# Group norm's factor by Ln and Exp on ScalarE instead of Sqrt and VectorE's reciprocal, in a layer of linear attention with a new table of turns

## The chip, the cores and the metric

The kernel runs on one core of one Trainium2 chip. A core has TensorE (PE in the rows; PEld is its loading of weights), VectorE (DVE), ScalarE (ACT), GpSimd (POOL) and SyncE (SP), which only issues transfers here. The time is the device time of one execution in microseconds; the figure for a kernel is the median of its runs.

## What is computed

Eight sequences of 256 tokens and 512 channels (32 heads of 16) pass through one layer of the RWKV kind. Everything is float32. Cut to what matters:

```python
xn = ln(x);  sx = shift(xn) - xn
x5 = xn + sx * (maa_stack + tanh((xn + sx * maa_x) @ maa_w1) @ maa_w2)      # five mixes
w  = exp(-exp(time_decay + tanh(x5[1] @ decay_w1) @ decay_w2))
r, k, v, g = x5[3] @ Wr.T, x5[0] @ Wk.T, x5[2] @ Wv.T, silu(x5[4] @ Wg.T)
for t in range(256):                                # state s: 16 x 16 for each head
    a = k_t v_t;  out_t = r_t (u * a + s);  s = a + w_t * s
m, var = mean and variance of out over the 16 channels of a head
att = (out - m) * rsqrt(var + 1e-5) * gn_w + gn_b   # the group norm: this factor is changed
x = x + att * g @ Wo.T
xn2 = ln(x);  x = x + sigmoid(xr @ ffn_Wr.T) * (square(relu(xk @ ffn_Wk.T)) @ ffn_Wv.T)
```

## The kernel before, in words

Each sequence b goes through three stages: `inputs_of_scan` (norm, mixes, the projections r, k, v, g and the decay w), `scan`, and `rest` (group norm, Wo, second norm and the feed-forward part). Channels lie on the 128 partitions, time along the free axis. The 512 channels are four blocks; each block is scanned in four pieces of 128 x 1024 (L1003, on VectorE). For a piece, v is written to DRAM (`vo`, L920 and L976), read back spread over partitions (`vs`), multiplied by k (L1001 on VectorE, six of them at L998 on GpSimd), scanned into `st8` (in the rows `st`), and multiplied by r on GpSimd (L1006). Four pieces are then summed over the channels of a head by 32 matmuls (`gather`, L1014).

All operations are first recorded as a list in `Plan`, each with an engine, an estimated duration and the buffers that it writes and reads. What decides the order on every engine is `TURNS`, a table written out by hand or by a search: one number for each operation, and among the operations that are ready the one with the lowest number is taken next (`sequence` and `order`). The transfers, issued by SP in one queue, stand in that order too. So do the activation tables: `tables` walks through ScalarE's operations and puts a load (L1170) ahead of one whose function is not in the table that is in place. PSUM holds six tiles `ps`, and one tile `wrep` of twice their bytes; SBUF tiles such as `vs` (six) and `st8` (six) rotate, and an operation that needs one waits for its last reader.

The stage `rest` begins with the group norm. The squares of `att` (`sq`, L1032) are averaged over each head by eight matmuls into `pv` (L1040). Line 1045 takes the root of `pv` plus eps on ScalarE, line 1051 the reciprocal on VectorE, in place in the tile `rs`, which is the first `sq` tile. For seven of the eight sequences sixteen copies of 32 partitions (L1073) spread the factor over the partitions, and GpSimd multiplies `att` by it (L1076). For the last sequence eight matmuls do the spreading (L1059) and VectorE multiplies (L1067). Scale and bias (L1080), the product with g (L1083, L1085) and the matmuls with Wo follow. A branch under `kept`, which is False, is never built.

At the start of the program the weights for v are centred: eight groups of matmuls multiply the raw v weights (`Wraw`, two loads of 512 KB) by a centring matrix `cen` of 64 KB. `xin` is the first mix, `ta` the tanh of its projection, `psm` the four mixes that come from it.

Of the kernel before, what the change touches and what calls it, by code (L numbers as in the profile page):

```python
# [68 lines left out]
class Plan:  # L69
# [10 lines left out]
              "sqrt": "sqrt_and_others"}  # L80
# [40 lines left out]
    def stage(self):  # L121
# [160 lines left out]
    def order(self, phases):  # L282
# [8 lines left out]
        while queue:  # L291
# [21 lines left out]
            if op.engine == "ACT":  # L313
                if want == "tanh" and now in ("exp", "silu"):
                    want = now
                elif now == "tanh" and want in ("exp", "silu"):
                    mode["ACT"] = now = want
# [928 lines left out]
```

## Time and profile before

| what | value |
|---|---|
| median of 3 runs | 606.35 us (605.95 to 607.21) |
| span of the profiled execution | 607.4 us |
| PE busy | 596.5 us, 98% of the span |
| DVE busy | 539.7 us, 89% |
| ACT busy | 519.0 us, 85% |
| POOL busy | 511.6 us, 84% |
| table loads on ACT | 34 of 1283 ns |

The profiled execution's time is its span, 607.4 us; no other time of it is listed, and it lies 1.05 us above the median of the unprofiled runs. Busy time is the union of an engine's instructions. An engine that is busy all the time need not be at its best pace: PE also counts as busy when its clock is halved.

### The profile page before, as it was taken

Reading aid. Unit: us, or ns where it says so; the run is one execution under the profiler, and the core shown is the slowest. Engines: PE = TensorE matmul, PEld = TensorE weight load, DVE = VectorE, ACT = ScalarE, POOL = GpSimd, SP = SyncE. Lnnn points to the kernel's source line nnn. Section 1 sums busy time; section 2 is a strip of 40 time slices with the busy share of each in tenths; the row PEclk is TensorE's granted clock in tenths of the full one; section 3 lists DMA queues with packets and bytes.
Section 4 is the critical chain, followed back from the end, with each engine's and each line's share of the span. In section 5 each row is a group of like instructions: output and inputs, shape, how many; then the busy total and the mean of one; then the engine's idle time right before and its main releaser. Section 6 shows DMA issues by size and latency. Waiting matters only on the chain.

```text
span 607.4 us, 17029 instructions
## 1 busy us (share of the span) xinstructions
PE 596.5 (98%) x7022; PEld 346.3 (57%) x7022; DVE 539.7 (89%) x492; ACT 519.0 (85%) x1177; POOL 511.6 (84%) x405
## 2 busy tenths in 40 slices
PE   9999998899999999999999999999999999999997
PEld 7575655347634774446654584465744474546464
DVE  5789999799999999998899999999899999995342
ACT  5977879979999999989999999999998899968350
POOL 2989999989979999899989899988889798987020
PEclk9999999799999999999999999999999999999999
DMA  9887695649668789669767987788667878972352
GB/s 316 272 198 209 184 253 170 167 119 284 193 162 227 198 250 244 182 191 253 202 196 214 269 215 213 210 256 216 166 184 195 231 202 216 282 206 74 130 187 77
DMA packets 52638, 124.73 MB, mean 205 GB/s; under 512 B 5841, under 2 KB 11345, under 8 KB 52561
## 3 DMA queue, kind: packets, MB, share of 16 engines
q1 hardware_dynamic: 48048, 119.39, 70.3%
q10 hardware_dynamic: 4512, 4.26, 2.2%
q8 instruction: 55, 0.90, 0.7%
q14 instruction: 23, 0.18, 0.1%
HBM read 115.25 MB, written 8.39 MB: 204 GB/s over the span
## 4 chain that ended last, share of the span: by engine, by line
PE 68%; POOL 14%; ACT 7%; DVE 5%; DMA 3%; issue 2%; SPq 0%; ACTq 0%; DVEq 0%; POOLq 0%
PE ps L440 57%; POOL st L1006 7%; PE ps L1014 7%; POOL mix L822 3%; PE ps L658 2%; POOL vs L998 1%; DVE st L1003 1%; DMA vo<-v 1%; PE ps L862 1%; PE ps L564 1%; DMA x<-in_x 1%; DMA vs<-vo 1%; DVE vs L1001 1%; ACT xh L595 1%; POOL mix L850 1%
## 5 line engine op out<-in xcount | busy, mean ns | idle before, releaser
L1003 DVE TENSOR_TENSOR_SCAN st<-wrep,vs 128x1024 f32<-128x1024 f32 x128 | 287.9, 2273 | 7.1 <-PE ps L1014 3.5
L1006 POOL TENSOR_TENSOR st<-st,r 128x1024 f32<-128x1024 f32 x128 | 254.8, 2008 | 7.4 <-DVE st L1003 6.0
L1001 DVE TENSOR_TENSOR vs<-vs,ps 128x1020 f32<-128x1020 f32 x122 | 142.6, 1199 | 2.0 <-ACT ps L980 1.0
L440 PE MATMUL ps<-Ws,mix 128*32 128x512 f32 (+3 forms) x872 | 115.1, 585 | 0.0
L440 PEld LDWEIGHTS ps<-Ws,mix 128*32 128x32 f32 (+1 forms) x872 | 37.5, 116 | 63.1 <-issue 58.5
L822 POOL TENSOR_TENSOR mix<-mix,xn 128x512 f32<-128x512 f32 x62 | 66.9, 1103 | 4.1 <-DVE mix L806 4.0
L1014 PE MATMUL ps<-st,con 128*32 128x256 f32 x1024 | 63.7, 388 | 2.4 <-POOL st L1006 1.6
L440 PE MATMUL ps<-mix,Wv 128*32 128x256 f32 (+1 forms) x832 | 59.5, 380 | 1.2 <-DVE mix L819 1.0
L440 PE MATMUL ps<-mix,Wk 128*32 128x256 f32 (+1 forms) x856 | 59.8, 380 | 0.0
L440 PE MATMUL ps<-mix,Wr 128*32 128x256 f32 (+1 forms) x712 | 59.2, 380 | 0.0
L440 PE MATMUL ps<-mix,Wg 128*32 128x256 f32 (+1 forms) x544 | 58.1, 380 | 0.1
L440 PE MATMUL ps<-Ws,g 128*32 128x512 f32 (+1 forms) x416 | 58.1, 606 | 0.0
L440 PE MATMUL ps<-mix,Ws 128*32 128x256 f32 (+1 forms) x688 | 57.8, 380 | 0.0
L1014 PEld LDWEIGHTS ps<-st,con 128*32 128x32 f32 x1024 | 33.1, 111 | 30.0 <-issue 9.0
L440 PEld LDWEIGHTS ps<-mix,Wg 128*32 128x32 f32 (+1 forms) x544 | 42.2, 133 | 12.8 <-issue 0.7
L440 PEld LDWEIGHTS ps<-mix,Wv 128*32 128x32 f32 (+1 forms) x832 | 36.6, 116 | 22.4 <-issue 3.0
L440 PEld LDWEIGHTS ps<-mix,Ws 128*32 128x32 f32 (+1 forms) x688 | 39.6, 123 | 16.7 <-issue 1.4
L440 PEld LDWEIGHTS ps<-mix,Wr 128*32 128x32 f32 (+1 forms) x712 | 38.8, 122 | 16.9 <-issue 1.3
L440 PEld LDWEIGHTS ps<-mix,Wk 128*32 128x32 f32 (+1 forms) x856 | 37.0, 115 | 19.8 <-issue 2.2
L804 ACT ACTIVATE ps<-ps,vec 128x256 f32<-128x256 f32 x112 | 45.5, 448 | 2.9 <-PE ps L440 2.0
L1170 ACT ACT_TABLE_LOAD x33 | 42.3, 1283 | 0.6
L736 POOL TENSOR_TENSOR mix<-mix,sx 128x512 f32<-128x512 f32 x28 | 35.5, 1279 | 6.6 <-ACT mix L729 3.7
(143 smaller groups left out, 1000.4 us busy)
## 6 DMA issues: line engine op xcount, KB each, us to landing
vs<-vo SPq DMA_DIRECT2D x128, 512.0 KB, 5.2
Ws<-in_wo SPq DMA_DIRECT2D x16, 512.0 KB, 5.4
Ws<-in_fk SPq DMA_DIRECT2D x16, 512.0 KB, 5.5
Ws<-in_fr SPq DMA_DIRECT2D x16, 512.0 KB, 5.7
Ws<-in_fv SPq DMA_DIRECT2D x16, 512.0 KB, 5.3
x<-in_x SPq DMA_DIRECT2D x9, 512.0 KB, 6.0
vo<-v ACTq DMA_DIRECT2D x15, 256.0 KB, 5.4
out<-o SPq DMA_DIRECT2D x15, 256.0 KB, 3.8
```

The costliest lines, as they stand in the source:

```text
L440: nc.tensor.matmul(out[i : i + n], lhsT=w[:, i : i + n], rhs=x, start=first, stop=final)
L564: nc.tensor.matmul(ps()[:, 0, :], lhsT=warm[:, 0, 0:P], rhs=warm[:, 0, 0:T], start=True, stop=True)
L595: summed(junk[n], mv, [src[n]], lambda n=n: nc.scalar.activation(junk[n](), src[n](), AF.Copy, accum_out=mv()[:, n, 0:1]), 0)
L658: nc.tensor.transpose(to[:, m, n * P : (n + 1) * P], xh[n]()[:, k * P : (k + 1) * P], idt())
L736: gp(512, t, [t, u], lambda t=t, u=u: nc.gpsimd.tensor_tensor(t(), t(), u(), ALU.add))
L804: act(256, p_, [p_, vec], lambda g=g, q=q, m=m, p_=p_: nc.scalar.activation(p_()[:, m, :], p_()[:, m, :], AF.Identity, bias=col(f"maa_{g}" ...
L822: gp(512, t, [t, xn[q]], lambda q=q, t=t: nc.gpsimd.tensor_tensor(t(), t(), xn[q]()[:, :, 1 : T + 1], ALU.add))
L1001: dve(4 * T, [vs], [vs, kp], lambda m=m, vs=vs, kp=kp: nc.vector.tensor_tensor(vs()[:, :, 1:T], vs()[:, :, 1:T], kp()[:, m : m + 1, 1:T].t ...
L1003: dve(4 * T, [st], [w, vs, first], lambda w=w, vs=vs, st=st: nc.vector.tensor_tensor_scan(st().rearrange("p n t -> p (n t)"), w().rearrang ...
L1006: gp(4 * T, st, [st, r], lambda m=m, st=st, r=r: nc.gpsimd.tensor_tensor(st(), st(), r()[:, m : m + 1, :].to_broadcast([P, 4, T]), ALU.mul ...
L1014: nc.tensor.matmul(pat()[32 * i : 32 * i + 32, 0, :], lhsT=con()[:, s : s + 32], rhs=done[i]()[:, j, :], start=(j == 0), stop=(j == 3),)
L1170: nc.scalar.preload_act_table_set(op.table)
```

## The change

Lines 1045 to 1051 become two activations on ScalarE. The first is the logarithm of the variance plus eps, the second the exponential of -0.5 times it, in place. Both are marked "ln", whose table `natural_log_exp_and_others` also serves a later `exp`, and two lines in `order` and `tables` let an `exp` keep that table when it is in place. VectorE's reciprocal of 128 x 256 goes, eight of them. The dead branch `kept` goes. All of `TURNS` is replaced, so the order of work changes on every engine and in SP's queue. ScalarE's program holds 34 table loads before and after.

```diff
     TABLES = {"exp": "exp_and_others", "tanh": "exp_and_others", "silu": "silu_and_others", "sig": "sigmoid_and_others",
-              "sqrt": "sqrt_and_others"}
+              "sqrt": "sqrt_and_others", "ln": "natural_log_exp_and_others"}
...
     TURNS = """
-        8 72 12 20 41 124 40 135 48 116 79 78 141 119 3 32 84 31 128 181 183 185 11 10 19 39 62 68 36 65 69 37
...
@@ in order
                 elif now == "tanh" and want in ("exp", "silu"):
                     mode["ACT"] = now = want
+                elif want == "exp" and now == "ln":
+                    want = now
@@ in tables
                 want = "silu" if want == "silu" else "exp"
+            elif want == "exp" and mode == "ln":
+                want = mode
@@ in rest
         act(256, rs, [pv, eh], lambda: nc.scalar.activation(
-            rs()[:, 0:T], pv()[:, 0, :], AF.Sqrt, bias=eh()[:, 0:1]), "sqrt", 1)
-        kept = False
-        if kept:
-            dve(256, [pv], [rs], lambda: nc.vector.reciprocal(pv()[:, 0, :], rs()[:, 0:T]), 6.25)
-        else:
-            dve(256, [rs], [rs], lambda: nc.vector.reciprocal(rs()[:, 0:T], rs()[:, 0:T]), 6.25)
+            rs()[:, 0:T], pv()[:, 0, :], AF.Ln, bias=eh()[:, 0:1]), "ln", 1)
+        act(256, rs, [rs], lambda: nc.scalar.activation(rs()[:, 0:T], rs()[:, 0:T], AF.Exp, scale=-0.5), "ln")
```

Three places show what the new turns move. The first is PE's order near the start, some 9 to 14 us into the run. `Ws_168` is the centring matrix, `Ws_169` the second half of the raw v weights; `mix_109` and `mix_110` are the two halves of `xin`, and the rows that read `ta_123` are the four mixes. Before:

```order
L440 MATMUL ps_177<-Ws_168,Ws_169 128x128 x2
L440 MATMUL ps_176<-Ws_168,Ws_169 128x128 x2
L440 MATMUL ps_173<-mix_109,mw_66 128x256 x2
L440 MATMUL ps_173<-mix_110,mw_66 128x256 x2
L440 MATMUL ps_174<-Ws_168,Ws_169 128x128 x2
L440 MATMUL ps_173<-ta_123,mw2a 128x256
```

And now, in the changed kernel, at the same place:

```order
L444 MATMUL ps_176<-Ws_168,Ws_169 128x128 x2
L444 MATMUL ps_177<-Ws_168,Ws_169 128x128 x2
L444 MATMUL ps_175<-Ws_168,Ws_169 128x128 x2
L444 MATMUL ps_173<-mix_109,mw_66 128x256 x2
L444 MATMUL ps_173<-mix_110,mw_66 128x256 x2
L444 MATMUL ps_173<-ta_123,mw2a 128x256
```

The last centring group moved from behind the projection of `xin` to ahead of it. In SP's queue, the load of the centring matrix moved too: it stood right behind the first half of the raw v weights, and it now stands behind the vectors `vec` and the initial state `s` of the second sequence.

The second place is GpSimd's order where the first scans arrive, 33 to 47 us into the run. `sx` are the differences of neighbouring tokens for the third sequence, `st` the scanned pieces of the first, `vs` the one piece that GpSimd multiplies by k. Before:

```order
L935 TENSOR_TENSOR rk_153<-r_128,k_125 128x512
L1006 TENSOR_TENSOR st_155<-st_155,r_128 128x1024
L690 TENSOR_TENSOR sx_106<-xn_101 128x512
L998 TENSOR_TENSOR vs_150<-vs_150,k_125 128x4x255
L1006 TENSOR_TENSOR st_156<-st_156,r_128 128x1024
L690 TENSOR_TENSOR sx_105<-xn_102 128x512
L822 TENSOR_TENSOR mix_120<-mix_120,xn_104 128x512
```

And now:

```order
L939 TENSOR_TENSOR rk_153<-r_128,k_125 128x512
L1010 TENSOR_TENSOR st_155<-st_155,r_128 128x1024
L694 TENSOR_TENSOR sx_105<-xn_102 128x512
L694 TENSOR_TENSOR sx_106<-xn_101 128x512
L1010 TENSOR_TENSOR st_156<-st_156,r_128 128x1024
L1002 TENSOR_TENSOR vs_151<-vs_151,k_125 128x4x255
L1010 TENSOR_TENSOR st_157<-st_157,r_128 128x1024
```

The second `sx` and one `st` moved ahead of `vs`. In SP's queue the second load of the g weights moved behind seven of the first eight `vs` transfers.

The third place is PE's order at the last group norm, about 559 to 568 us. `L1040` and `L1044` are the averages into `pv`, `L1059` the spreading of the factor, the rows that read `Ws_168` with a `mix` are the feed-forward projection of the sequence before. Before:

```order
L1040 MATMUL ps_173<-sq_162,con 32x256 x2
L440 MATMUL ps_175<-Ws_168,mix_117 32x512 x8
L440 MATMUL ps_175<-Ws_169,mix_119 32x512 x8
L1059 MATMUL ps_173<-sq_161,con 128x256
L1059 MATMUL ps_172<-sq_161,con 128x256
```

And now:

```order
L1044 MATMUL ps_177<-sq_161,con 32x256 x2
L444 MATMUL ps_173<-Ws_168,mix_114 32x512 x8
L1059 MATMUL ps_177<-sq_162,con 128x256
L1059 MATMUL ps_172<-sq_162,con 128x256
L444 MATMUL ps_173<-Ws_170,mix_110 128x512 x2
```

One half of that projection moved from between the averages and the spreading to behind the spreading. A little later, the two halves of the last sequence's Wo product for its first 128 tokens now follow one another, where before they alternated with the second 128 tokens.

## Rows read from the trace of the kernel before

**Rows 1.** The page: busy time, share of the span and instructions of each engine.

```profile
PE 596.5 (98%) x7022; PEld 346.3 (57%) x7022; DVE 539.7 (89%) x492; ACT 519.0 (85%) x1177; POOL 511.6 (84%) x405
```

**Rows 2.** Stretches of 15 us: busy us by engine, granted clock, DMA share, GB/s.

```profile
0.00:15.00 15.00, 13.78 (x86) 11.76 (x90) 8.44 (x24) 8.19 (x19) 4.02 (x20) 1.00 0.92 315
...
90.00:105.00 15.00, 13.15 (x232) 7.90 (x228) 15.00 (x14) 13.90 (x30) 15.00 (x12) 1.00 0.70 197
105.00:120.00 15.00, 12.23 (x190) 6.51 (x184) 10.81 (x11) 14.21 (x33) 15.00 (x10) 0.85 0.58 147
...
255.00:270.00 15.00, 15.00 (x216) 6.89 (x212) 13.08 (x12) 13.32 (x32) 14.97 (x11) 1.00 0.65 186
```

**Rows 3.** PE's waits, whole run: for whom, us in total, times, longest.

```profile
PE ps L440 <- ACT k L901: 1.2, 1, 1.2
```

**Rows 4.** Groups by line: shapes, count, busy us, mean ns, idle before.

```profile
L1170 ACT ACT_TABLE_LOAD x33 | 42.3, 1283 | 0.6
...
L1051 DVE RECIPROCAL sq<-sq 128x256 f32<-128x256 f32 x8 | 13.9, 1736 | 2.5 <-ACT sq L1045 2.5
...
L1045 ACT ACTIVATE sq<-ps,eh 128x256 f32<-128x256 f32 x8 | 3.8, 474 | 0.3 <-PE ps L1040 0.3
L781 ACT ACTIVATE ta<-ps 128x256 f32<-128x256 f32 x8 | 3.0, 380 | 1.6 <-PE ps L440 1.6
```

**Rows 5.** PE's instructions in order of time, start: start, duration, idle before.

```profile
8.01 3.36 PE L440 MATMUL ps<-Ws,Ws 128*128 128x128 f32 x28
11.20 1.96 PE L440 MATMUL ps<-mix,mw 128*128 128x256 f32 x8
13.00 0.61 PE L440 MATMUL ps<-Ws,Ws 128*128 128x128 f32 x4
13.63 1.15 PE L440 MATMUL ps<-ta,mw2a 32*128 32x256 f32 x16
```

**Rows 6.** SP's transfers in order of time: start and duration of the issue.

```profile
2.10 0.47 SPq L429 DMA_DIRECT2D Ws<-in_consts  x1
2.61 0.43 SPq L429 DMA_DIRECT2D vec<-in_vecs  x1
...
4.07 1.05 SPq L429 DMA_DIRECT2D s<-in_state  x1
...
24.05 14.35 SPq L429 DMA_DIRECT2D vs<-vo  x8
```

**Rows 7.** Transfers, whole run: size, median us from issue to landing.

```profile
Ws<-in_consts SPq DMA_DIRECT2D x1, 64.0 KB, 5.2
```

**Rows 8.** POOL's instructions in order of time, 36 to 47 us.

```profile
38.70 2.37 POOL L998 TENSOR_TENSOR vs<-vs,k 128x1020 f32<-128x1020 f32 x1 [1.44 <-DMA vs<-vo]
41.02 2.00 POOL L1006 TENSOR_TENSOR st<-st,r 128x1024 f32<-128x1024 f32 x1
42.98 1.05 POOL L690 TENSOR_TENSOR sx<-xn 128x512 f32<-128x512 f32 x1
```

**Rows 9.** A stretch of 2 us around PE's wait for POOL, columns as above.

```profile
116.00:118.00 2.00, 1.74 (x20) 0.82 (x24) 0.81 (x3) 1.98 (x7) 2.00 (x3) 0.50 1.02 242
```

**Rows 10.** PE in order of time: first g projection, two summing groups, a Wo product.

```profile
47.90 5.39 PE L440 MATMUL ps<-mix,Wg 128*32 128x256 f32 x96
53.11 1.91 PE L1014 MATMUL ps<-st,con 128*32 128x256 f32 x32
...
116.26 3.64 PE L1014 MATMUL ps<-st,con 128*32 128x256 f32 x32 [1.59 <-POOL st L1006]
119.67 8.32 PE L440 MATMUL ps<-Ws,g 128*32 128x512 f32 x64
```

**Rows 11.** PE in order of time, at the last group norm and after.

```profile
559.62 3.62 PE L440 MATMUL ps<-Ws,mix 128*32 128x512 f32 x32
563.17 1.13 PE L1059 MATMUL ps<-sq,con 64*128 64x256 f32 x8
...
578.89 1.09 PE L658 MATMUL ps<-idt,xh 128*128 128x128 f32 x8 [0.40 <-DVE xh L628]
```

More of the change, by code (lines that the diff above doesn't have):

```diff
@@ L1072, in rest @@
                         rows = slice(32 * i, 32 * i + 32)
-                        act(335 if kept else 376, rsb, [pv if kept else rs], lambda blk=2 * q + n, n=n, rows=rows, rsb=rsb: nc.scalar.copy(
-                            by_block(rsb)[rows, n, :],
-                            (pv()[:, 0, :] if kept else rs()[:, 0:T])[32 * blk : 32 * blk + 32, :]))
+                        act(376, rsb, [rs], lambda blk=2 * q + n, n=n, rows=rows, rsb=rsb: nc.scalar.copy(
+                            by_block(rsb)[rows, n, :], rs()[32 * blk : 32 * blk + 32, 0:T]))
                 gp(512, att, [att, rsb], lambda att=att, rsb=rsb: nc.gpsimd.tensor_tensor(
```

269 rows, old and new, of the table TURNS are left out of this document.

## Prediction

> **What bounds the kernel now.** I read the page's busy times first. PE is busy for 596.5 us, DVE for 539.7, ACT for 519.0 and POOL for 511.6 [rows 1]. The span is 607.4 us, so PE is idle for 10.9 us in all, and work taken from another engine can give back at most what PE waits for it, or what PE loses to its clock. So the next question is where PE's idle time lies, and the stretches of 15 us answer it. In the long middle PE is busy for all 15.00 us of a stretch while DVE has 13.08 and ACT 13.32 [rows 2]: there PE is the bound. In the first stretch PE lacks 1.22 us, and from 90 to 120 us it lacks 1.85 and 2.77 us, while POOL is busy for all of 30 us [rows 2]: in the first fifth of the run POOL's queue paces PE. The list of waits names what is left: PE's wait at the summing group at 116.26 us is for POOL, 1.59 us long [rows 10], and one of 1.2 us is for an evacuation by ACT [rows 3]. Behind the wait at 116 us comes a second loss. The granted clock is 0.50 there, the lower level of 1.2 GHz [rows 9]; the 32 matmuls take 3.64 us where the same group took 1.91 us, and the 64 behind them 8.32 us [rows 10] where 32 of that shape take 3.62 us [rows 11], so 2 x 3.62 = 7.24. The lower clock costs 1.73 + 1.08 = 2.8 us.
>
> **What the change removes.** Eight reciprocals of 1.736 us, 13.9 us of DVE [rows 4]. On the path I count them at nothing: in the middle PE's own work covers them, and in the stretch from 90 to 120 us it is POOL that is full. If DVE were the engine waited for, they would give up to 13.9 us, but DVE is the releaser of no wait of PE of that size, and after 116 us PE has no idle time to give.
>
> **What it adds.** Eight exponentials of 128x256 on ACT. No row shows this one; the nearest are the tanh of the same shape at 0.380 us and the root at 0.474 us [rows 4], and I take 0.38, since the tanh too has no pointer for its bias: 3.0 us of ACT's 607. The step from variance to factor shrinks from 0.474 + 1.736 us on two engines to 0.474 + 0.38 on one. Queued behind the exponential on ACT stand a table load and then copies out of PSUM that PE waits for. I take nothing for it, because PE's work covers ACT's 13.32 of 15 us [rows 2]; without that cover seven exponentials in the middle would cost 7 x 0.38 = 2.7 us. That end is kept for the range.
>
> **Table loads.** A load takes 1.283 us [rows 4], and the built programs hold 34 before and after, since a tanh follows the new pair and wants the other table back. So the term is nothing. The Trainium skill (ScalarE: Activation LUTs, section "Table sets: the hidden batching unit") says that a logarithm followed by an exponential needs one load where an exponential and a root need two. By that rule ACT would lose eight loads, 10.3 us, and the third rival below would fall away; by the order of this kernel it loses none, and no run shows otherwise yet.
>
> **The new turns, start.** At 8.01 us PE begins the centring of the v weights; 28 of its matmuls stand before the projection of xin at 11.20 us, four behind it, and the tanh of that projection releases the four mixes at 13.63 us [rows 5]. Now all 32 stand before it. From 8.01 to 11.20 us is 3.19 us for 28, so 3.65 for 32: the projection, and all that follows from it, starts 0.46 us later. That is the lower end. The centring matrix is also issued later. Before, its issue was at 2.10 us [rows 6] and it landed 5.2 us later [rows 7], at 7.3, before PE asked for it. Now the issues of vec (0.43) and of the state (1.05) [rows 6] go first: about 3.65, landing at 8.85, so 0.84 us behind 8.01. Upper end 1.3 us. The state's 1.05 us may be less in a queue that is less full, so I take the middle, +0.9 us. Behind the delayed mixes stand the projections of v, its way through DRAM, and the first scans.
>
> **The new turns, POOL.** At 38.70 us POOL has waited 1.44 us for a transfer of vs [rows 8]. The row at 42.98, an sx of 1.05 us, and the st at 41.02, 2.0 us [rows 8], now go ahead of that vs, so the transfer may land some 3 us later before POOL waits. Gain 1.44 us, at least 1.05 if the st is late itself; I take 1.44, since the 3 us of work that go ahead of vs are twice the gap. POOL then stays full until 120 us [rows 2], the work ahead of the summing group at 116 us is the same set of instructions on POOL and on PE in both kernels, and so this group starts 1.44 - 0.9 = 0.54 us earlier, with PE's wait before it and the lower clock behind it unchanged. After it PE is the bound and carries the 0.54 us to the end.
>
> **Transfers that move.** The second half of the g weights goes behind seven vs transfers, issued by 24.05 + 14.35 = 38.4 us at the latest [rows 6]. Its first reader is at 47.90 us [rows 10], 9.5 us later, and the one landing shown here took 5.2 [rows 7]. Nothing, and at most a wait of PE at that place, which POOL's pace would swallow until 116 us.
>
> **The new turns, end.** Between the last averages and the spreading stood two halves of a projection, 3.62 us of PE [rows 11], enough to hide the root and the reciprocal (2.2 us). Now one half, 1.8 us, stands there and 0.85 us of ACT are to be hidden: no wait, no gain, since the other half only moves. At 578.89 us PE waits 0.40 us for the normed tokens [rows 11]. The first 128 tokens' Wo product is now finished before the second's begins, so one of the two statistics is out of the way early: I take the 0.40 us, between 0 and 0.4.
>
> **Sum.** +0.9 - 1.44 - 0.40 = -0.94 us: 606.5 in the profiled span. The span of before lies 1.05 us above the median of 606.35, and I move the median by the same sum: **605.4 us**. With the ends of the terms: 0.46 - 1.44 - 0.40 = -1.4 and 1.3 - 1.05 - 0 = +0.25, so 605.0 to 606.6.
>
> **Rivals.** First, the clock does not fall. PE's idle time around 114 us is made of waits for ACT and for POOL; if the new order splits it so that the granted clock stays at 2.4 GHz, the 2.8 us come back: 605.4 - 2.8 = 602.6. For it speaks that both waits lie in one short stretch and any shift of ACT's evacuations divides them anew; against it that their sum is set by POOL, which has the same work. The Trainium skill (TensorE: Matmul & The Clock Gate, Part 1) says that the moment at which the clock switches varies from run to run of the same kernel. By that rule a run could come out at this rival's 602.6 without any cause in the program; the one trace here shows one fall after a wait, which agrees, and cannot show the variation.
>
> Second, the start costs its upper end and POOL gains nothing, because the first scans come 1.3 us late and POOL, which now wants two of them before vs, waits for DVE instead of for the transfer: +1.3 - 0.4 = +0.9, 607.2. Against it: DVE loses work at the same time only later, but its first multiplication waits for a transfer that is no longer behind the g weights.
>
> Third, on the other side: the exponentials come to stand in front of PSUM copies that PE needs. PE already waited 1.2 us for ACT at one such copy [rows 3]. If seven exponentials each reach PE with their 0.38 us, 605.4 + 2.7 = 608.1. It decides from the point where PE waits for ACT at six of the seven places (6 x 0.38 = 2.3 us takes 605.4 past 607.6). Against it: DVE's results reach ACT 1.36 us sooner at the same places.
>
> **How the numbers follow.** I give the forecast 0.50, the clock 0.20, the lost POOL gain 0.13, the ACT waits 0.17. A change of 0.2%, 1.2 us, is about what a measurement of this kernel can tell from none; that is 605.1 and 607.6. Within 0.2%: the lost gain and two thirds of the forecast, 0.46. Faster: the clock and one third of the forecast, 0.37. Slower: the ACT waits, 0.17. The range reaches to the clock's 602.6 and the ACT waits' 608.1, which leaves out about one in ten on either side; the forecast's own is 605.0 to 606.6.
>
> **What the changed profile would show.** The mixes' first matmuls at about 14.5 us instead of 13.63; no wait of POOL for the transfer near 38 us; the summing group now at 116.26 at about 115.7 us, with a clock of 0.50 behind it; no RECIPROCAL of 128x256, and an exponential near 0.38 us; 34 table loads; no wait at the last transposes. The prediction is wrong if the clock column has no 0.50 near 116 us or has a second one, or if PE's waits for ACT after 130 us add up to more than 1 us.

## The result, and the profile after

The changed kernel takes 608.34 us in the median of 5 runs (608.07 to 609.51); the kernel before took 606.16 us in 5 runs of the same comparison (605.9 to 607.21). The ratio is 1.0037, with a 95% interval of 1.0021 to 1.0052: the change makes the kernel 2.2 us slower, where 1 us faster was forecast.

The two profiled spans hide this, 607.4 us before and 607.7 after. In every execution that lists both, the time is 1.8 us more than the span, so the profiled execution of before would have been listed at 609.2 us, 2.9 above the median that the prediction was made from. It was an unlucky one, and that matters below. One execution of the run e4 below was in a slower state (626.87 us at a granted clock of 0.949) and is left out of its figures.

The page's busy times of the changed kernel, against [rows 1]:

```profile
PE 594.6 (98%) x7250; PEld 347.1 (57%) x7250; DVE 530.8 (87%) x484; ACT 522.5 (86%) x1185; POOL 512.2 (84%) x405
```

DVE loses 8.9 us and ACT gains 3.5. The groups by line answer to [rows 4] (count, busy us, mean ns, idle before):

```profile
L1169 ACT ACT_TABLE_LOAD x33 | 42.3, 1283 | 0.6
L1049 ACT ACTIVATE sq<-ps,eh 128x256 f32<-128x256 f32 x8 | 3.8, 474 | 0.1
L1051 ACT ACTIVATE sq<-sq 128x256 f32<-128x256 f32 x8 | 3.3, 416 | 0.2
```

No load is added, the logarithm costs what the root cost, and the exponential 0.416 us where 0.38 was forecast. Of these, nothing explains a loss. The stretches of 15 us of the changed kernel, columns as in [rows 2], say where to look:

```profile
45.00:60.00 15.00, 13.34 (x244) 8.10 (x237) 13.60 (x14) 9.94 (x22) 15.00 (x12) 1.00 0.80 229
60.00:75.00 15.00, 15.00 (x278) 12.11 (x272) 13.96 (x10) 12.78 (x26) 12.67 (x9) 1.00 0.70 187
...
105.00:120.00 15.00, 12.36 (x206) 8.26 (x202) 12.56 (x12) 14.29 (x34) 15.00 (x11) 0.92 0.71 179
```

The same two stretches of the kernel before:

```profile
45.00:60.00 15.00, 14.87 (x272) 8.78 (x268) 15.00 (x14) 10.62 (x24) 15.00 (x13) 1.00 0.79 214
60.00:75.00 15.00, 15.00 (x276) 9.10 (x272) 15.00 (x11) 13.42 (x28) 15.00 (x10) 1.00 0.65 173
```

The prediction has POOL full up to 120 us. It is not: from 60 to 75 us POOL is busy for 12.67 of 15.00 us, and from 45 to 60 us PE for 13.34, where it had 14.87. POOL's instructions of the changed kernel in order of time (start, duration, idle before) show the wait of [rows 8] gone, and two new ones:

```profile
40.48 2.39 POOL L1002 TENSOR_TENSOR vs<-vs,k 128x1020 f32<-128x1020 f32 x1
...
60.08 2.02 POOL L1002 TENSOR_TENSOR vs<-vs,k 128x1020 f32<-128x1020 f32 x1
63.30 1.09 POOL L972 TENSOR_TENSOR att<-v,att 128x512 f32<-128x512 f32 x1 [1.20 <-ACT att L967]
...
71.54 3.96 POOL L1010 TENSOR_TENSOR st<-st,r 128x1024 f32<-128x1024 f32 x2 [1.12 <-DVE st L1007]
```

Each is followed back one step. ACT's instructions of the changed kernel:

```profile
53.99 0.30 ACT L998 ACTIVATE vs<-s,cm 128x4 f32<-128x4 f32 x1 [2.55 <-DMA vs<-vo]
54.19 0.58 ACT L984 COPY ps<-k 128x512 f32<-128x512 f32 x1
54.79 1.28 ACT L1169 ACT_TABLE_LOAD   x1
56.09 1.08 ACT L935 ACTIVATE g<-ps 128x512 f32<-128x512 f32 x2
```

ACT stands still for 2.55 us before an instruction of 0.30 us that writes four columns of a vs tile, because that tile's transfer has not landed. Behind it in ACT's queue stand a copy, a table load and both evacuations of g, and, later, the copies of att for which POOL waits at 63.30. In the kernel before, the write of this piece stood behind both evacuations. The wait at 71.54 comes by way of DVE, whose instructions of the changed kernel show two waits in a row, the second for a transfer:

```profile
59.16 4.47 DVE L1007 TENSOR_TENSOR_SCAN st<-wrep,vs 128x1024 f32<-128x1024 f32 x2 [1.40 <-ACT vs L998]
64.68 2.34 DVE L1005 TENSOR_TENSOR vs<-vs,ps 128x1020 f32<-128x1020 f32 x2 [1.04 <-DMA vs<-vo]
66.94 4.46 DVE L1007 TENSOR_TENSOR_SCAN st<-wrep,vs 128x1024 f32<-128x1024 f32 x2
```

The transfers that SP issues in the changed kernel at that time (start of the issue, duration):

```profile
49.40 1.80 SPq L433 DMA_DIRECT2D vs<-vo  x3
51.25 0.58 SPq L433 DMA_DIRECT2D x<-in_x  x1
51.92 0.42 SPq L433 DMA_DIRECT2D Ws<-in_wo  x1
55.60 6.41 SPq L433 DMA_DIRECT2D vs<-vo  x2
```

A load of x and one of half of Wo now stand ahead of the vs transfer that is issued at 55.60 us and for which DVE waits until 64.68. The kernel before issued an x load ahead of 39 us and its first Wo load behind 73 us.

PE's instructions of the changed kernel show what arrives there, against [rows 5] and [rows 10]:

```profile
13.97 1.15 PE L444 MATMUL ps<-ta,mw2a 32*128 32x256 f32 x16 [0.68 <-ACT ta L785]
...
56.78 1.93 PE L1018 MATMUL ps<-st,con 128*32 128x256 f32 x32 [1.66 <-POOL st L1010]
...
117.55 3.53 PE L1018 MATMUL ps<-st,con 128*32 128x256 f32 x32 [1.28 <-POOL st L1010]
```

The summing group that stood at 116.26 us stands at 117.55, where 115.7 was forecast. From the terms: 0.34 for the start, -1.44 for the wait of POOL that went, 1.20 + 1.12 for those that came, gives +1.22 us, and 1.29 are measured, with the same set of instructions on POOL up to the group's last piece in both programs. (The wait at 56.78 is put down to POOL, but its pieces were done at 47.8 us. The program gives this group the PSUM tile of the first g projection, and ACT empties that from 56.09 on: this is ACT's late evacuation again. By PE's wait ACT's copies of att come late, and so POOL's wait at 63.30.)

### The profile page after: what moved, and what is told of

It reads as the page before. It is cut to its first block, busy times and chain, and to the rows that moved or that the text cites. A ratio compares the mean times of both kernels' runs of the same rounds, so it can differ in the third digit from the quotient of the medians.

```text
span 607.7 us, 17471 instructions
## 1 busy us (share of the span) xinstructions
PE 594.6 (98%) x7250; PEld 347.1 (57%) x7250; DVE 530.8 (87%) x484; ACT 522.5 (86%) x1185; POOL 512.2 (84%) x405
## 4 chain that ended last, share of the span: by engine, by line
PE 71%; DVE 13%; POOL 7%; DMA 3%; ACT 2%; issue 2%; SPq 0%; DVEq 0%; ACTq 0%; POOLq 0%
PE ps L444 60%; PE ps L1018 7%; DVE st L1007 6%; DVE vs L1005 4%; POOL st L1010 4%; DMA vs<-vo 3%; PE ps L662 2%; DVE mix L810 2%; PE ps L866 1%; POOL mix L826 1%; POOL vs L1002 1%; DMA xt<-in_x 1%; DVE x L1090 0%; PE ps L1044 0%; ACT L1169 0%
## 5 line engine op out<-in xcount | busy, mean ns | idle before, releaser
L444 PEld LDWEIGHTS ps<-mix,Wv 128*32 128x32 f32 (+1 forms) x856 | 37.9, 115 | 20.0 <-DVE mix L823 1.6
L444 PEld LDWEIGHTS ps<-mix,Ws 128*32 128x32 f32 (+1 forms) x784 | 37.8, 118 | 19.2 <-issue 1.4
L810 DVE TENSOR_TENSOR mix<-ps,sx 128x512 f32<-128x512 f32 x56 | 36.3, 678 | 4.2 <-ACT ps L808 2.7
```

Of the source, the lines that this page charges most:

```text
L444: nc.tensor.matmul(out[i : i + n], lhsT=w[:, i : i + n], rhs=x, start=first, stop=final)
L810: dve(512, [t], [p_, sx[q]], lambda q=q, t=t, p_=p_: nc.vector.tensor_tensor(t(), p_(), sx[q](), ALU.mult))
```

## The experiments

`MOVED` in the diffs gives an operation, named by its number in `TURNS`, another number; a fraction puts it between two others.

| run | what it is | median, us (runs) | ratio to before, 95% interval | median of the runs at granted clock 1.00 (runs) |
|---|---|---|---|---|
| e1 | arithmetic alone, old turns | 613.76 (5) | 1.0110 (1.0094 to 1.0127) | 612.4 (2) |
| e2 | new turns alone, old arithmetic | 632.55 (4) | 1.0430 (1.0413 to 1.0447) | none |
| e3 | changed kernel, ACT's write later | 608.92 (9) | 1.0039 (1.0023 to 1.0056) | 608.0 (3) |
| e4 | e3, and the loads put back | 606.98 (11) | 1.0002 (0.9987 to 1.0016) | 605.8 (5) |
| e5 | the loads put back alone | 607.62 (12) | 1.0012 (1.0000 to 1.0025) | 607.1 (8) |
| e6 | kernel before again | 607.14 (12) | 1.0003 (0.9988 to 1.0018) | 605.0 (1) |
| e7 | kernel before with both faults | 607.33 (12) | 1.0006 (0.9989 to 1.0023) | 605.7 (2) |
| e8 | old turns, copies for reciprocals | 608.03 (12) | 1.0017 (1.0000 to 1.0033) | 605.9 (3) |
| e9 | changed kernel again | 609.05 (10) | 1.0047 (1.0030 to 1.0064) | 608.3 (3) |
| e10 | e4, and PE's start put back | 606.82 (12) | 0.9999 (0.9986 to 1.0013) | 606.0 (5) |
| e11 | e10, and three of POOL's later | 607.04 (12) | 1.0009 (1.0000 to 1.0018) | 606.9 (4) |
| e12 | kernel before, POOL's step alone | 607.15 (12) | 1.0015 (0.9999 to 1.0031) | 605.3 (1) |

The kernel before took 606.52 us in the comparison of e1 to e4 (20 runs), 606.83 in that of e5 to e8 (35), 606.39 in that of e9 to e11 (27) and 606.45 in that of e12 (17). Its runs at a granted clock of 1.00 had medians of 605.5 (7), 605.8 (9), 605.6 (7) and 604.9 us (6) in these four.

### Arithmetic and turns apart: e1 and e2

e1 is the change without its lines of `TURNS`:

```diff
-            rs()[:, 0:T], pv()[:, 0, :], AF.Sqrt, bias=eh()[:, 0:1]), "sqrt", 1)
-            dve(256, [rs], [rs], lambda: nc.vector.reciprocal(rs()[:, 0:T], rs()[:, 0:T]), 6.25)
+            rs()[:, 0:T], pv()[:, 0, :], AF.Ln, bias=eh()[:, 0:1]), "ln", 1)
+        act(256, rs, [rs], lambda: nc.scalar.activation(rs()[:, 0:T], rs()[:, 0:T], AF.Exp, scale=-0.5), "ln")
```

> The logarithm and the exponential in the order of the kernel before. In that order five more table loads fall on ACT (38 in place of 33, because the roots of the layer norms shared the root's table with the group norm): ACT gets 5 x 1.28 + 8 x 0.4 = 9.6 us more, DVE 13.9 us less. Theory (the loss comes from the new turns between 50 and 75 us): the arithmetic moves the time by less than 0.2%, 605.0 to 607.4, and POOL still waits about 1.4 us for a transfer near 38.7 us. Rival (the exponentials, or the loads, stand in front of PSUM copies that PE needs): 608 or more, with PE's waits for ACT adding up to more than 1 us behind 130 us.

613.76 us, 7.2 above the kernel before: the theory, that the arithmetic moves the time by less than 0.2%, falls, and the rival came (PE's waits for ACT behind 130 us add up to 4.2 us). The groups by line of this run count five loads more:

```profile
L1169 ACT ACT_TABLE_LOAD x38 | 48.8, 1283 | 0.6
```

and its stretch from 300 to 480 us, columns as in [rows 2], shows PE without work for 5.4 us of 180, where the second trace of the kernel before has 179.92 us of work:

```profile
300.00:480.00 180.00, 174.62 (x2166) 98.74 (x2161) 163.21 (x136) 168.87 (x380) 159.64 (x124) 1.00 0.75 208
```

The reason that the expectation gives for the five loads, a table shared with the layer norms' roots, is not the right one: in the kernel before each of the eight roots of the group norm has a load of its own. ACT's instructions of e1 show what happens (L1049 is the logarithm, L1051 the exponential, L1108 a tanh):

```profile
301.00 0.47 ACT L1049 ACTIVATE sq<-ps,eh 128x256 f32<-128x256 f32 x1
...
301.88 1.28 ACT L1169 ACT_TABLE_LOAD   x1
303.18 1.09 ACT L1108 ACTIVATE o<-ps 128x512 f32<-128x512 f32 x2
304.28 1.28 ACT L1169 ACT_TABLE_LOAD   x1
305.57 0.42 ACT L1051 ACTIVATE sq<-sq 128x256 f32<-128x256 f32 x1
```

In the old order a tanh stands between the two steps at three of the eight places (the others at 380 and 444 us), so the table is changed there and back, which makes five loads more in all. At 309.09 us PE then waits 1.40 us for the next tanh on ACT. In the changed kernel no load stands between the two steps anywhere.

e2 is the other half, the change's lines of `TURNS` with the root and the reciprocal.

> The new order with the root on ACT and the reciprocal on DVE. Theory: the new turns alone make the loss, so 608.3 within 0.6, with ACT standing still until about 54.0 us for a transfer of vs, and POOL's waits at about 63.3 and 71.5 us. Rival (arithmetic): back at 606.2. If the reciprocals on DVE hurt in this order too (DVE is what POOL waits for at 71.5 us), up to 610.

632.55 us, far above everything that was expected. DVE's instructions of this run show how one place comes about:

```profile
161.96 0.42 DVE L1020 TENSOR_TENSOR att<-ps,att 128x256 f32<-128x256 f32 x1 [1.19 <-PE ps L1014]
167.71 1.75 DVE L1051 RECIPROCAL sq<-sq 128x256 f32<-128x256 f32 x1 [5.32 <-ACT sq L1045]
169.38 4.41 DVE L1003 TENSOR_TENSOR_SCAN st<-wrep,vs 128x1024 f32<-128x1024 f32 x2
```

The reciprocal stands in DVE's queue ahead of scans that were ready, and DVE waits 5.32 us for the root before it. At 180.04 us PE then waits 6.28 us for DVE. So neither half can be run with the other's partner: the new turns are made for a factor that DVE has no part in, the old ones put a tanh between the logarithm and the exponential.

### Do ACT's wait and the loads make the loss: e3, e4, e5

e3 moves the write of four columns behind both evacuations of g; e4 also issues the loads of x and Wo where the kernel before had such loads; e5 moves the loads alone.

```diff
+    MOVED = {268: 281.5}                              # e3
+    MOVED = {268: 281.5, 278: 218.5, 285: 346.6}      # e4
+    MOVED = {278: 218.5, 285: 346.6}                  # e5
...
-                op.rank = int(t)
+                op.rank = self.MOVED.get(int(t), int(t))
```

> The changed kernel with one number of its order changed: the first-column write of vs0_2_2 on ACT, which stands still 2.55 us until 53.99 us, goes behind the two evacuations of g. Theory (this wait is where the loss starts): the evacuations begin at about 52 in place of 54 us, PE's wait of 1.66 us at 56.78 goes, and the time falls by 1 to 2 us, to 606.3 to 607.3. Rival (the loads of x and Wo ahead of a vs transfer make the loss at 63 and 71 us): 607.8 or more, POOL's waits at 63.3 and 71.5 us stay as they are.

> As the one before, and the loads of x (at 51.25 us) and of the first half of Wo (51.92 us) are issued where the kernel before had such loads: x at about 38.5 us, Wo behind the vs transfers of the first sequence, at about 70 us. Theory (both together are the loss between 50 and 75 us): no wait of POOL over 0.6 us between 40 and 75 us, the summing group of 117.55 us comes at 115.5 or earlier, and the time is 605.0 to 606.4. Rival (the two medians differ because the clock falls in one kernel's runs and not in the other's): 608.3 still, though the waits are gone.

> The changed kernel with only the loads of x and of the first half of Wo issued where the kernel before had them; the first-column write stays where ACT waits for it. The run with the write and the loads moved was 2.4 us below the changed kernel at a granted clock of 1.00 (605.76 and 608.16 us). Theory (two waits of POOL, 1.20 us at 63.30 us from ACT's wait and 1.12 us at 71.54 us from the loads, add up): POOL keeps about 1.2 us at 63 us and loses none at 71 us, 606.9 at that clock, between the two. Rival 1 (the loads are all of it): 605.8. Rival 2 (the waits cover one another, so that only both moves help): 608.2.

What POOL waits for at 71 us is the pair of scans that starts at 66.94 us in the changed kernel. DVE's rows of that pair in e3, with the multiplications ahead of it:

```profile
64.50 2.34 DVE L1007 TENSOR_TENSOR vs<-vs,ps 128x1020 f32<-128x1020 f32 x2 [1.70 <-DMA vs<-vo]
66.77 4.46 DVE L1009 TENSOR_TENSOR_SCAN st<-wrep,vs 128x1024 f32<-128x1024 f32 x2
```

in e5, with the scans ahead of it:

```profile
58.99 4.47 DVE L1009 TENSOR_TENSOR_SCAN st<-wrep,vs 128x1024 f32<-128x1024 f32 x2 [1.26 <-ACT vs L1000]
...
65.61 4.46 DVE L1009 TENSOR_TENSOR_SCAN st<-wrep,vs 128x1024 f32<-128x1024 f32 x2
```

and in e4:

```profile
64.51 4.47 DVE L1009 TENSOR_TENSOR_SCAN st<-wrep,vs 128x1024 f32<-128x1024 f32 x2
```

Against e4 the pair is 1.10 us late with ACT's write alone (e5), 2.26 with the loads alone (e3), and 2.43 with both (the changed kernel): each covers the other's delay. That is why e3 gains nothing that can be measured (POOL's wait at 63 us is gone, the one at 71 us has grown from 1.12 to 1.81), and its rival was right about the time, though not about the waits, which did not stay as they were. e5 comes out between, 607.1 at a granted clock of 1.00 where 606.9 was expected, but not by the way expected: the wait at 63 us is the one that went, since with the loads moved the program also gives the group at 56.78 another PSUM tile, and 1.08 us are left at 70 us. e4 has neither wait. POOL's instructions of e4:

```profile
61.98 1.10 POOL L974 TENSOR_TENSOR att<-v,att 128x512 f32<-128x512 f32 x1
...
69.12 3.96 POOL L1012 TENSOR_TENSOR st<-st,r 128x1024 f32<-128x1024 f32 x2
73.05 2.37 POOL L1004 TENSOR_TENSOR vs<-vs,k 128x1020 f32<-128x1020 f32 x1
```

The vs at 73.05 us came at 75.47 in the changed kernel, 2.42 us later. At a granted clock of 1.00 e4 takes 605.8 us, where the changed kernel took 608.2 in the first comparison and 608.3 in e9's: 2.4 us again. With the kernel before e4 is level (1.0002), so these two causes are the whole loss as far as the interval, 0.9 us to either side, can tell.

### Are these waits the program's, or one execution's: e6 and e9

Both kernels ran again, unchanged.

> The kernel before, unchanged, for a second trace and for its time by granted clock. Theory (the fall of the clock near 116 us is in some executions and not in others, for the same program): executions at 1.00 take about 605.7, those at 0.997 about 606.7, those at 0.994 about 607.8, and a trace at 1.00 shows no 0.50 near 116 us. Rival (the fall belongs to the program's waits): every execution shows it.

> The changed kernel once more, unchanged, because a second trace of the kernel before did not show the wait of 1.44 us at 38.70 us on which the prediction rested. Theory (the waits between 50 and 75 us belong to the new order): ACT stands still for 2 to 3 us near 54 us, POOL's waits between 60 and 75 us add up to 1.8 to 2.6 us, the summing group comes at about 117.5 us, 608.2 at a granted clock of 1.00 and 608.9 at 0.997. Rival (they were the accident of one execution too): POOL's waits there add up to less than 1 us, and the median is 607 or less.

The second trace of the kernel before, POOL in order of time:

```profile
37.04 2.35 POOL L998 TENSOR_TENSOR vs<-vs,k 128x1020 f32<-128x1020 f32 x1
```

and PE:

```profile
114.72 3.33 PE L1014 MATMUL ps<-st,con 128*32 128x256 f32 x32 [1.47 <-DVE cm L941]
```

e6's own question, on the clock, is taken up in the last section. The wait of 1.44 us [rows 8], the largest term of the prediction, isn't there: vs starts at 37.04 in place of 38.70 us, and the summing group at 114.72 in place of 116.26. In five traces with that order (these two, e1, e7, e8) the wait is 1.44, 0, 0.71, 0 and 0 us. The second trace of the changed kernel has the new waits again, on POOL:

```profile
63.26 1.10 POOL L972 TENSOR_TENSOR att<-v,att 128x512 f32<-128x512 f32 x1 [1.22 <-ACT att L967]
...
71.22 3.97 POOL L1010 TENSOR_TENSOR st<-st,r 128x1024 f32<-128x1024 f32 x2 [0.84 <-DVE st L1007]
```

and a median of 609.05 us, as its theory had it. Against this second trace of the kernel before, the summing group of the changed kernel is 117.55 - 114.72 = 2.83 us late, and no longer 1.29. So the wait that the change removed was mostly an accident, and the waits that it brought are not.

### The term by itself: e12

```diff
+    MOVED = {223: 208.5, 210: 222.5}
```

This is the kernel before with POOL's vs behind the sx and the st, and nothing else.

> The kernel before, with one step of the change alone: POOL's sx and st go ahead of the vs for which POOL waited 1.44 us at 38.70 us in the profiled execution. The prediction's term: that wait goes in every execution, 1.44 us less, so 605.0 against 606.4. Theory now (of five traces in that order of POOL and of the transfers the wait was 1.44, 0.71, 0, 0 and 0 us long, 0.43 in the mean): no wait for that transfer in the trace, and the median falls by 0.4 or less, 606.0 to 606.4. Rival (the st or the sx that now stand ahead are late themselves): slower by up to 1 us, with a wait of POOL for DVE or ACT between 36 and 40 us.

POOL's instructions of this run:

```profile
37.59 1.04 POOL L692 TENSOR_TENSOR sx<-xn 128x512 f32<-128x512 f32 x1 [0.58 <-ACT xn L683]
38.59 2.00 POOL L1008 TENSOR_TENSOR st<-st,r 128x1024 f32<-128x1024 f32 x1
40.55 2.39 POOL L1000 TENSOR_TENSOR vs<-vs,k 128x1020 f32<-128x1020 f32 x1
```

No wait for the transfer, but one of 0.58 us for ACT in its place, and no gain: 1.0015 (0.9999 to 1.0031). The prediction's term of -1.44 us does not show in the median.

### The arithmetic's own price: e8

```diff
-            dve(256, [rs], [rs], lambda: nc.vector.reciprocal(rs()[:, 0:T], rs()[:, 0:T]), 6.25)
+        act(256, rs, [rs], lambda: nc.scalar.copy(rs()[:, 0:T], rs()[:, 0:T]))
```

> The order of the kernel before, with a copy of 128x256 on ACT in the place of the eight reciprocals on DVE; the factor is then the root and not its inverse, which this kernel leaves out. Against the run of the logarithm and the exponential in that order (613.76) this has no more table loads than the kernel before. Theory (five loads of 1.28 us and what they push made that run's 7.2 us, the eight short instructions on ACT cost nothing and the eight reciprocals gave nothing): the kernel before's time within 0.8. Rival 1 (the exponentials themselves stand in front of PSUM copies): 609 or more. Rival 2 (DVE's 13.9 us were worth something): 605 or less.

This kernel leaves the inverse out, so its factor is the root. 608.03 us, 1.2 above, with an interval from 0 to 2.0 us, a little over what was expected; its trace shows only 0.2 us of it behind the summing group (489.9 us to the end against 489.7 in the second trace of before). Taken with e1, whose 7.2 us differ from this run by the five loads and nothing else of size, the loads made most of e1's loss. The eight reciprocals that DVE no longer has to do gave nothing.

### Three tries that missed: e7, e10 and e11

e7 was to give the kernel before both faults:

```diff
+    MOVED = {309: 282.5, 293: 277.5, 269: 298.3, 362: 298.6}
```

> The kernel before, given both faults on purpose: ACT's first-column write of a vs that lands at 56.2 us goes ahead of the first evacuation of g, at about 53.3 us, and the loads of x and of the first half of Wo go ahead of the vs transfer that is issued at 56.86 us. Theory: ACT stands still for about 2.9 us, DVE waits for that vs, POOL gets waits of 1 to 2.5 us between 60 and 75 us, and the time is 607.5 to 609, 1 to 2.5 us over the kernel before. Rival (these waits lie beside other work and the loss of the changed kernel is elsewhere): the kernel before's time within 0.5.

The faults didn't arise. With the load of x behind the vs transfers these landed sooner, and ACT's write ran at 53.41 us without a wait. The loads, issued at 49.54 and 50.22 us, took 8.5 and 9.6 us to land, so they were still on their way when the next vs was issued at 56.93 us; but DVE's multiplications at 61.18 us started without a wait. It says nothing on the theory.

e10 puts TensorE's first groups back on top of e4, e11 also moves three of POOL's instructions later, to find a version under both kernels:

```diff
+    MOVED = {268: 281.5, 278: 218.5, 285: 346.6, 44: 37.05, 40: 37.1, 41: 37.2, 47: 37.3, 49: 39.5, 46: 53.5, 48: 45.2, 50: 45.4}   # e10
+    (the same, and) 476: 531.5, 538: 572.3, 569: 635.5    # e11
```

> The run with the write and the loads moved, and TensorE's first groups in the order of the kernel before: the centring of the third and fourth quarter of the v weights first, one group of four matmuls behind the projection of xin. Theory (the copy of the third quarter, a table load of 1.28 us and the tanh stand behind one another on ACT, and so the mixes come 0.4 us late): the tanh at about 13.0 in place of 13.45 us, the summing group of 115.29 us at 114.9, 605.4 at a granted clock of 1.00 against 605.8. Rival (POOL's wait for r at 33 us is set elsewhere): the start is earlier, the group and the time stay.

> As the run with the start put back, and three of POOL's instructions that nobody needs yet go later: a multiplication of vs for the second sequence (2.1 us) behind the pieces of the summing group of 115 us, and a mix and an att product (1.1 us each) behind the pieces of the next one or two groups. Theory (POOL alone paces TensorE from 60 to 130 us): that summing group comes about 1.5 to 2 us earlier, and the time is 603.4 to 604.4 at a granted clock of 1.00, under both kernels. Rival (DVE's scans or the copies of r on ACT take POOL's place at once): the group moves by less than 0.5 us and the time is 605.2 or more.

In e10 the second half of the raw v weights, which the new turns load later, comes late: at 9.45 us PE waits 0.49 us for it, the mixes start at 14.15 us, not earlier, and the summing group stands at 116.08 us. In e11 it stands at 115.17 us, 0.91 earlier than in e10, which is between its theory (1.5 to 2 us) and its rival (less than 0.5), and two new waits of PE behind it follow, 0.68 us for DVE at 124.65 and 1.25 us for POOL at 150.08. Both theories of these runs fell; no version here is measurably faster than the kernel before.

## Why the prediction was wrong

**The step that failed** is "I take 1.44, since the 3 us of work that go ahead of vs are twice the gap. POOL then stays full until 120 us", and the sentence that hangs on it, "so this group starts 1.44 - 0.9 = 0.54 us earlier". It failed twice. The wait of 1.44 us belonged to one execution; four other traces in that order have 0 to 0.71 us (e6), and its removal alone gains nothing (e12). And POOL did not stay full: the same set of instructions, in another order on ACT and on SP's queue, gave it waits of 1.20 and 1.12 us at 63 and 71 us, which come back in a second trace (e9) and whose removal brings back 2.4 us (e4). The second rival, that POOL gains nothing, was nearest in kind, but by another way than the one it named. In number the third (608.1) was nearest, but its mechanism did not come: behind 130 us PE has no wait for ACT in this trace. None of the signs of being wrong that the prediction lists came either (one fall of the clock, no such waits); they did not test the step that failed.

**Transfers that move** were counted at "nothing", after only the g weights had been looked at. They did no harm; the loads of x and Wo, which go ahead of a vs, were missed.

**Start, +0.9 us**: the mechanism's first half was right, since PE's group of 28 became 32 and grew from 3.36 to 3.74 us. The upper half did not come: the issue of the state took 0.43 us in this queue, not 1.05, and the centring began at 7.82 us. The mixes start 0.34 us later [rows 5], with a piece that was not foreseen, a wait of 0.68 us for a tanh that stands behind two copies and a table load on ACT.

**Reciprocals and exponentials at nothing, table loads at nothing**: right for the change as made. In the changed kernel's trace one thing alone waits for the exponential, a weight load, 0.8 us at the last group norm. But the loads stay at 34 only by the new turns: in the old ones (e1) the same arithmetic has 39. The order, and not the functions alone, sets their number. The Trainium skill (ScalarE: Activation LUTs, section "Table sets: the hidden batching unit") lets a logarithm and an exponential share one load; here the pair does where nothing comes between (all eight places of the changed kernel), and the count still rises by five in e1, where a tanh comes between.

**End, -0.40 us**: right in size, and that by luck. PE's instructions of the kernel before, against [rows 11]:

```profile
559.19 0.61 PE L1040 MATMUL ps<-sq,con 128*32 128x256 f32 x8
...
579.82 3.60 PE L440 MATMUL ps<-Ws,mix 128*128 128x512 f32 x8
```

and of the changed kernel:

```profile
559.84 0.61 PE L1044 MATMUL ps<-sq,con 128*32 128x256 f32 x8
...
578.83 1.44 PE L662 MATMUL ps<-idt,xh 128*128 128x128 f32 x8
580.10 3.60 PE L444 MATMUL ps<-Ws,mix 128*128 128x512 f32 x8
```

From the averages of the second half at 559.84 to the product behind the transposes it is 20.26 us; in the kernel before, from 559.19 to 579.82, 20.63. But the wait for the normed tokens did not go. It stands in the weight loads of the transposes, which now begin after the first half of the tokens and wait once more for the second:

```profile
578.82 0.14 PEld L662 LDWEIGHTS ps<-idt,xh 128*128 128x128 f32 x1 [0.77 <-DVE xh L632]
579.28 0.75 PEld L662 LDWEIGHTS ps<-idt,xh 128*128 128x128 f32 x7 [0.32 <-DVE xh L632]
```

Nor is one of the two statistics early: DVE takes both in one go at 576.17 us, behind the second half of the Wo product, as it did before at 575.78. From the product ahead of the transposes to the one behind them it is 4.81 us where it was 4.92, so 0.11 us of the 0.37 come there; the other 0.26 come ahead of it and were not traced further. The gain of 0.37 is lost again elsewhere behind 120 us: from the summing group to the end the changed kernel takes 490.2 us at a clock of 0.997, the second trace of before 489.7. PE's wait of 0.41 us for a mix of POOL at 152.56 us is the largest piece of it; the rest was not traced.

**The clock**: the row with 0.50 is there, behind 118 us in place of 116. But the first rival, that the clock does not fall, holds in part of the executions of every kernel, before and after, so it is no matter of the change. And the sum was made against a span that carried the longest fall (a mean granted clock of 0.994, in 8 of 111 executions) and the accidental wait, then moved onto a median whose fall is mostly shorter (0.997) and whose wait is mostly shorter or absent.

## What to carry to other kernels

One trace shows one execution. A wait for a transfer that is the main term of a forecast should be seen in a second trace before it is taken away, and its queue's neighbours read in both; a wait that the order of an engine's own queue makes, such as that of an instruction of 0.30 us that holds ACT for 2.55, came back in both further traces that have this order (2.56 us in e9, 2.42 in e5). An order that was searched for one set of instructions belongs to that set: half of such a change, run by itself, tells little of the whole (1.011 and 1.043 for the halves, 1.0037 together). When a table of turns is replaced, every load that passes a transfer on the same queue needs a look, the ones of other sequences too.

## What the hardware showed that was not expected

The same program has executions with a mean granted clock of 1.00, 0.997 and 0.994, and what that costs can be read from the summing group to the end of the span:

| trace | group at, us | span, us | from group to end | clock |
|---|---|---|---|---|
| before, shown ahead | 116.26 | 607.4 | 491.1 | 0.994 |
| before again (e6) | 114.72 | 604.4 | 489.7 | 0.997 |
| changed | 117.55 | 607.7 | 490.2 | 0.997 |
| changed again (e9) | 117.23 | 607.4 | 490.2 | 0.997 |
| e4 | 115.29 | 605.2 | 489.9 | 0.997 |
| e3 | 117.40 | 606.2 | 488.8 | 1.000 |
| e5 | 116.25 | 605.2 | 489.0 | 1.000 |
| e12 | 115.16 | 603.4 | 488.2 | 1.000 |

A step of the clock is about 1 to 1.5 us, though PE's two waits just ahead of the group add up to much the same in all of them, 2.5 to 2.9 us. The theory of e6 holds, as far as traces at 1.00 exist: none is of the kernel before itself, but e3, e5 and e12 have 1.00 and no 0.50 near 116 us. In e12 the group itself shows it, 1.93 us for the 32 matmuls that took 3.64 [rows 10]:

```profile
115.16 1.93 PE L1016 MATMUL ps<-st,con 128*32 128x256 f32 x32 [1.61 <-POOL st L1008]
```

The Trainium skill (TensorE: Matmul & The Clock Gate, Part 1) says that the moment of the switch varies from run to run; these runs agree, with 33 of 111 listed executions of the kernel before at 1.00 or 0.999 and the rest at 0.994 to 0.997.
